# Two graph layers on one core: the table's rows fetched and weighted in three parts, and a rewritten steady list

## The chip, the core and the metric

The kernel runs on one core of a Trainium2 chip. The metric is the device time in microseconds (us) of one execution; the time of a kernel is the median of its runs. The core's engines each work through their own queue in order: TensorE (PE; PEld are its weight loads), VectorE (DVE), ScalarE (ACT), GpSimd (POOL) and SyncE (SP), which here issues DMAs only. They wait for each other through semaphores.

## What is computed

Input x has 32 batches of 512 channels by 1024 nodes; adj is 512 by 512. The reference, cut to what matters:

```python
def layer0(x, wq, wk, adj, bm):
    q = einsum('c,bcn->bn', wq, x)
    k = einsum('c,bcn->bn', wk, x)
    scores = q[:, None, :] + k[:, :, None]
    scores = where(scores > 0, scores, 0.01 * scores)
    att = softmax(scores, axis=-1)
    agg = einsum('bcn,bmn->bcm', x, att)
    return relu(einsum('oc,bcm->bom', adj, agg) + bm[None, :, None])

x = layernorm(x + layer0(x, wq, wk, adj, bm))
W = adj * adj
x = layernorm(x + einsum('bnf,nm->bmf', x, W) + bias)
```

## The kernel before

The score of a pair is a leaky ReLU of q + k, so the softmax needs no matrix of 1024 by 1024: with the nodes ranked by q, the nodes above a threshold get one exponential factor and those below another, and the weighted sum is a running sum from either end of the ranking. For each batch the kernel therefore does the following.

- **Projections p0 to p27** (`project`, L329): adj times x by a Strassen-like scheme with seven products, for two halves g of the nodes, in fp32. The order of the products is in `order` (L298): p0, p1 are P2, p2, p3 are P1, p4, p5 are P5, p6, p7 are P6, p8, p9 are P3, p10, p11 are P7 and p14, p15 are P4 of the first half; p12, p13 and p16 to p27 belong to the second half. Each accumulates into one of the PSUM banks A (P1, P6, P7, P4), B (P5, P3) and C (P2). A step named in NARROW (L934) issues its weights as two loads of 64 columns, each with its own matmul into half of the output; another issues one load of 128. Steps k (`keep`, L347) read a bank out to `zrow`, on ScalarE or VectorE: k0p1, k0p5, k0u2, k011, k022, k012 and k021 for the first half. Until k0p5 has copied P5 out of B, p8 and p9 may not accumulate there; p2 and p3 need A to be free of the batch before (`rd21`, the last read of the final product).
- **Ranking**: qb spreads q over the partitions, r0 to r7 (L403) count ranks on VectorE, sd0 to sd7 (L415) scatter the rows on GpSimd by indirect DMA into a table `td` in DRAM, c0 to c7 (L428) count thresholds on ScalarE.
- **Fetch** (fe, `fetch`, L454): SyncE reads the ranked rows back into `zs`, NB = 9 blocks of 60 rows for each half of the partitions. Block 8 takes two small DMAs (L461); the others come in three pairs (L466): blocks 0 and 1, block 7, blocks 2 to 6.
- **Weights of the table** (wx, wb): wx0 and wx1 (`weigh_exp`, L476, ScalarE, two Exp each) and wb0 and wb1 (`weigh_by`, L488 and L496, VectorE) make the triangular weights `lq`. Part 0 covers blocks 7, 8 and 0, 1 and part 1 the rest.
- **Table t0 to t8** (`table`, L510): running sums by matmul; step s takes block 8-s from above and block s from below. e (L522) evicts it on ScalarE, ca (ScalarE) and cp (GpSimd, both L528) carry its border rows into the next blocks, and ts (L536) stores it to `td` by DMA. A table step needs the carries of the step before, and so its e.
- **Gather** pi0 to pi7 (L543, GpSimd, indirect DMA) brings each node's three table rows into `rows`; oa, ox and no (L558 to L575) make the mixing factors; sc (L582, ScalarE) and ga, gb (L587, VectorE, "gains") mix the three.
- **Back**: u0 to u3 (L596) transpose the mixed rows, ad (L603) adds x, sq, rt, y (L612, L619, L628) are the first layer norm; rt is GpSimd's. u0 reads all eight node tiles, so it needs every gain.
- **Second layer**: T1 to T4 (L652) and m0 to m13 (L676) are a second Strassen-like product; m6, m7 need y2 and y3. rd reads the banks out, st, ro, sf, av (L705 to L729) are the second layer norm, so stores and ld loads the next x.

Nothing is scheduled by a tool here. Three lists written out by hand give the order of the program: BEGIN (L855), SLOT (L921), which is passed 28 times and where each step belongs to one of five batches in flight, and END (L885). Each engine gets its steps in the list's order; every engine waits in its own queue. The pool of PSUM has the banks A, B and C, and T for the table.

Of the kernel before, what the change touches and what calls it, by code (L numbers as in the profile page):

```python
# [23 lines left out]
def gat_gcn_resnorm_kernel(  # L24
# [25 lines left out]
    NB = N // R + 1  # L50
# [403 lines left out]
    def fetch(b):  # L454

        zd = tdb[b % 2].rearrange("(s u) c -> s u c", u=3)
        full = zd[0 : (NB - 1) * R, 0, :].rearrange("(j q p) c -> q p j c", q=2, p=RH)
        for half in range(2):
            r = (NB - 1) * R + half * RH
            n = min(RH, N - r)  # L460
            nc.sync.dma_start(  # L461
                out=zs[half * G + 1 : half * G + 1 + n, NB - 1, 0:ZW], in_=zd[r : r + n, 0, :]
            )
        for j0, j1 in ((0, 2), (NB - 2, NB - 1), (2, NB - 2)):
            for half in range(2):
                nc.sync.dma_start(  # L466
                    out=zs[half * G + 1 : half * G + 1 + RH, j0:j1, 0:ZW],
                    in_=full[half, :, j0:j1, :],
                )

    some_blocks = (((NB - 2, NB), (0, 2)), ((0, NB - 2), (2, NB)))
# [9 lines left out]
    def weigh_by(b, part, by=nc.vector):  # L481

        w = weights(b)
        for i, (j0, j1) in enumerate(some_blocks[part]):
            if part == 1:
                j0, j1 = max(j0, 1), min(j1, NB - 1)
# [7 lines left out]
        if part == 1:  # L494
# [267 lines left out]
    def also(role, name, f, *at):  # L762
        steps[name] = role, f, at
# [22 lines left out]
    also(1, "sx", share_exp)  # L786
    for h in range(2):
        also(1, f"wx{h}", weigh_exp, h)
        also(1, f"wb{h}", weigh_by, h)
# [72 lines left out]
    @0 fe @1 k022 p17 @0 sb1 @1 p14 k1p5 p15 @0 sb2 sg @1 p21 k021 p19 @0 c0 @1 p18 p20 k1p1 @0 c1 @1  # L862
    k111 p22 p23 @0 wx0 wb0 t0 @2 x11 @1 k1u2 @2 x12 @1 p25 @2 x03 @0 e0 @1 p24 k112 @0 ca0 ts0 cp0
    c2 t1 @1 k122 @0 wx1 @1 qb @0 wb1 e1 @1 p27 @0 ts1 @1 ql @0 cp1 @1 pk @0 c3 @1 p26 r0 @2 p4 @1
    k121 r1 @0 c4 @1 en @0 ca1 t2 @1 r4 @0 c5 @1 sd1 r5 @2 p5 @0 e2 ca2 @1 mx @0 ts2 cp2 @1 mr @0 c6
    @1 sd4 @0 t3 @1 r2 @2 p2 @1 sd0 r3 @0 e3 ca3 ts3 cp3 @1 r6 @0 t4 @2 p1 @1 sd5 r7 @0 e4 ca4 cp4
    @1 sd3 @0 t5 @2 p3 @1 sd7 @0 e5 ts5 @2 k0p1 @0 cp5 ca5 @1 sd2 @0 t6 @2 p0 @0 e6 @2 k0p5 @0 cp6
    ts6 @2 k011 @0 ca6 @1 sd6 @0 t7 @2 x13 x14 p6 @0 e7 @2 p7 @0 ca7 cp7 ts7 t8 ts4 @2 k0u2 p11 @0
    e8 c7 @2 p10 @0 ts8 @1 fe @0 sh @2 k022 x04 p14 @0 qw3 pi0 @2 p15 p9 @1 wx0 wb0 @2 k021 @1 c0 @2
    p18 @1 t0 c1 @2 p19 @1 c2 @2 p8 @1 e0 ca0 cp0 ts0 @2 k012 @1 c3 @0 pi2 @2 k1p1 @0 pi1 @2 p22 @0  # L870
    pi3 @2 p23 @0 pi7 @2 p17 @0 pi5 @2 k1u2 p16 @1 c4 @0 pi6 @1 t1 @2 k1p5 @1 wx1 @0 pi4 @2 p24 @1
    wb1 c5 @2 p20 p12 p25 p21 p13 @0 oa0 ox0 sx no0 @2 k122 @0 sc0 @2 k112 @1 e1 @2 p27 @0 ga0 sc2
    @1 ts1 ca1 cp1 @0 sc1 gb0 @1 t2 @0 ga1 gb1 @1 e2 @0 sc3 @2 k111 @1 cp2 ca2 @0 ga2 @1 t3 @0 ga3
    gb3 @2 p26 @0 oa1 @1 e3 @0 ox1 @1 cp3 @0 no1 gb2 sc4 sc5 ga4 sc6 ga5 @1 ca3 @0 ga6 sc7 @1 t4 @0
    gb5 @1 c6 @0 ga7 gb4 gb7 @1 e4 @0 gb6 u0 @1 ca4 ts4 @2 k121 @1 cp4 ts3 c7 @0 ad0 @1 t5 ts2 @0 u1
    @1 sh e5 @0 sq0 u2 @1 cp5 @0 ad1 @1 ca5 t6 @0 rt0 @3 ld0 @2 en @0 ad2 sq1 @2 pk @0 u3 @1 e6 @3
    ld1 @2 mx @1 ca6 cp6 @0 sB @2 mr @0 sq2 rt1 ad3 @1 t7 @0 qw5 @3 ld2 @1 e7 @0 sA @1 ts6 @0 rt2 y0
    @2 qb @1 ts5 cp7 ca7 @2 r0 @1 ts7 t8 @0 sq3 @2 r1 @1 e8 @0 rt3 y1 m1 @1 ts8 @2 r2 sd1 @3 ld3 @2
    ql r3 sd0 @0 y2 m0 @2 r4 sd2 @0 y3 m7 qw4 @2 c0 @1 pi3 @0 T1 m6 @2 c1 r5 @1 pi2 @0 rdp1 m2 @1
    pi1 @0 T2 @2 c2 r6 @1 pi0 @0 m5 @2 c3 @0 T3 m4 T4 @3 x01 @0 m3 @2 r7 @0 rdu2 rd11 m9 @2 sd7 @0  # L880
    rdp5 @1 sx @2 c4 sd5 @0 m8 @1 pi5 @0 m11 rd22 @2 sd4 @0 m10 @1 pi6 oa0 ox0 @2 c5 @1 no0 @2 sd3
    @0 m13 @3 x02 @1 sc2 @3 x03 @1 sc1 @2 sd6 @0 rd12 @1 sc0 @0 m12 @3 x04 @1 pi7 @0 rd21 @1 pi4 @2
    c6 c7 @1 sc3 @2 fe
# [5 lines left out]
    @28 st2 @29 sc6 @30 wx0 @31 p15 @29 sc7 @30 wb0 @28 ro2 @30 t0 @31 k021 @29 sc4 @28 ro1 sf2 @31  # L889
    x12 p18 @29 ga6 @30 e0 @31 p19 @30 ca0 @31 k012 @30 ts0 cp0 @29 gb3 @30 t1 @31 k1p1 @29 ga7 sc5  # L890
    @31 p16 @29 gb7 @30 e1 @31 p12 @28 sf1 @30 wx1 cp1 ts1 ca1 @31 p17 @30 wb1 @28 so3 av1 @30 t2
    @29 ga4 ga5 @31 p23 @30 e2 sh @31 p22 k1p5 @30 cp2 @31 k111 @30 ca2 t3 @29 gb4 @31 k1u2 @29 gb6
    @31 p25 @30 e3 @29 gb5 @30 ca3 @29 u0 @30 cp3 @28 av2 @30 t4 @29 ad0 @28 so2 @31 p24 @30 e4 @31
    x14 @30 ca4 @29 u1 @30 ts4 cp4 @31 k122 @29 sq0 @30 ts2 t5 @29 ad1 @28 so0 @31 p20 @30 e5 ca5
    @29 u2 @30 cp5 @29 sq1 @30 t6 @29 ad2 @31 p21 @30 e6 ca6 @29 u3 @30 cp6 ts6 @31 k112 @29 sq2 @30
    ts3 @31 pk @30 t7 @29 ad3 @28 so1 @31 p27 @30 ts5 e7 ca7 @31 mx @30 cp7 ts7 @31 qb mr @29 rt0
    @30 t8 @31 ql r0 @29 rt1 @31 p26 @30 e8 @31 r1 @29 sB @30 ts8 @31 k121 @29 y0 @31 en @29 sA @31
    r2 sd1 @29 sq3 @31 r3 sd0 @29 y1 m0 @30 pi3 @31 r4 c0 @30 pi2 @31 r5 @29 m1 @30 pi0 @29 T1 rt3
    @31 r6 @29 m2 rt2 @31 r7 sd2 @29 y2 m3 @31 sd3 @30 sx @29 rdp5 @30 pi1 @29 y3 m11 @31 sd5 @29
    rdp1 T2 @31 c1 sd7 @29 m5 @31 c2 sd6 @29 m7 @31 c3 sd4 @29 m10 @30 pi7 pi5 @29 m6 @30 oa0 ox0  # L900
    no0 @29 m4 T3 @30 sc3 sc0 @29 rd11 @31 fe @29 rdu2 T4 @31 c4 @29 m9 @30 sc2 @31 c5 @29 m8 @31 c6
    @29 rd22 @30 sc1 @31 c7 @29 rd12 m13 st0 @31 wx0 wb0 t0 @30 ga3 ga0 ga1 @31 e0 ca0 @29 st1 @31
    ts0 cp0 @30 pi6 @31 t1 @30 gb1 @29 m12 @31 e1 @30 gb3 @31 ca1 ts1 cp1 wx1 @29 ro0 @31 wb1 @29
    rd21 @31 t2 @30 pi4 ga2 @29 sf0 st2 @31 e2 ca2 cp2 t3 e3 ca3 cp3 @29 av0 ro1 @31 t4 @29 sf1 @30
    gb0 @31 e4 cp4 @30 oa1 ox1 @31 ca4 t5 @30 no1 gb2 sc4 sc5 ga4 sc7 ga5 @31 e5 @30 ga7 sc6 @31 cp5
    ca5 @30 ga6 @31 t6 @29 av1 @30 gb4 gb6 @29 so1 @30 gb5 @31 e6 @30 gb7 u1 @31 ca6 ts6 @29 st3 @31
    cp6 @29 ro2 @31 ts4 t7 ts2 @30 u0 @31 e7 ts3 ca7 @30 u3 @31 cp7 ts7 t8 @30 ad0 @31 ts5 e8 @30
    ad1 sq0 @31 ts8 @30 u2 @29 sf2 @31 sh @29 so0 @30 sq1 rt0 ad2 @31 sx @30 ad3 sq2 @31 pi0 @30 sA
    y0 rt1 @31 pi1 @30 y1 m1 @31 pi3 @30 sq3 T1 @31 pi2 @30 m0 rt2 sB rdp1 rt3 m3 y2 @31 pi7 @30 y3
    m7 @31 pi5 @30 T2 m6 @31 pi4 @30 T4 @31 pi6 @30 T3 m4 @29 ro3 @31 oa0 @30 m5 @31 ox0 no0 @30  # L910
    rd11 @31 sc2 @30 m2 rdu2 @31 ga2 sc3 @30 m9 @31 gb2 sc1 sc0 ga1 @30 rdp5 m8 @31 ga3 ga0 @29 av2
    @31 gb3 @30 m11 rd22 @31 gb0 @30 m13 @31 oa1 ox1 no1 @30 m12 @31 gb1 sc4 sc7 ga4 @30 m10 @31 sc5
    ga7 @30 rd21 @31 gb4 gb7 sc6 ga5 ga6 gb5 gb6 u0 @30 rd12 @31 u1 ad0 u2 sq0 ad1 u3 ad2 sq1 rt0
    ad3 sB y0 rt1 @30 st0 @31 sA y1 m0 @29 sf3 @31 sq2 @30 ro0 @31 T1 m1 sq3 rt2 m3 y2 rt3 y3 m2
    rdp1 T2 m6 rdp5 @30 st1 @29 av3 @31 m5 @30 sf0 st2 ro1 @31 m4 T4 @30 ro2 @31 T3 m7 rdu2 @30 sf1
    @31 rh110 @30 av1 st3 @31 m8 @30 so1 sf2 @29 so2 @30 ro3 av2 @29 so3 @31 m9 rh220 @30 av0 @31
    rh111 hb21 m10 rh221 @30 sf3 @31 hb31 @30 av3 @31 m11 rh120 @30 so3 @31 st0 @30 so0 so2 @31 m12
    rh121 ro0 st1 m13 rh210 sf0 hb20 ro1 av0 sf1 ag2 rh211 so0 ro2 av1 hb30 ag3 sf2 ro3 fa21 so1
    fa20 fo20 sf3 fa31 fa30 fo21 fo31 fo30
    """  # L920
    SLOT = """  # L921
    st1 p4 st0 p2 ga2 p5 ro0 st3 p3 p0 k0p1 ga0 k0p5 ro3 p1 st2 ro1 p7 ga3 p6 ro2 gb2 p8 sf3 k0u2
    sf0 ga1 av3 p10 gb0 k011 p11 x13 p12 oa1 k022 p9 ox1 av0 no1 p14 gb3 sc7 k012 p15 wx0 wb0 t0 x11
    k021 ga7 sc4 p19 sf1 gb1 e0 p17 ca0 ts0 sf2 cp0 sc6 x12 t1 av1 ga6 p16 gb6 e1 p18 wx1 cp1 ts1
    ca1 wb1 p13 so1 k1p1 sc5 t2 ga4 gb7 p22 e2 x14 p23 ca2 k111 cp2 ga5 t3 k1u2 k1p5 gb5 p24 gb4 e3
    ca3 u0 ts3 cp3 av2 so3 t4 ad0 so2 p21 so0 e4 ts2 ca4 u1 cp4 sq0 t5 ad1 p20 ld0 e5 ca5 u2 cp5 ts5
    sq1 rt0 t6 ad2 p25 ld1 rt1 e6 y0 u3 ts6 k122 cp6 k112 p26 ca6 pk ad3 sq2 t7 p27 e7 ld2 mx cp7
    ts7 k121 qb mr ca7 rt2 en ts4 y1 t8 r0 sA e8 r1 sB sq3 ts8 m0 sh sd0 ql ld3 T1 m1 c0 sd1 r2 m3
    rdp1 pi3 r3 y2 m2 rt3 r4 pi2 y3 m6 pi0 c1 T2 m7 sx pi1 T4 rdp5 c2 T3 m4 c3 pi5 r5 m5 r6 sd5 m11
# [47 lines left out]
```

## Times and profile before

| what | value |
|---|---|
| median of 3 runs | 2200.91 us (2197.12 to 2201.44) |
| the profiled execution: whole run | 2198.41 us |
| its span, first to last instruction | 2196.7 us |
| mean granted clock of TensorE | 0.99 |
| instructions | 35479 |
| DMA | 548.86 MB, mean 250 GB/s |

The page gives busy times and their share of the span by engine, then the chain of work that ended last: followed back from the last instruction, at each step to what released it. A timeline row has the start and the length in us, the engine, the line, the operation, the tile written and read with their shapes, the number of records, and in brackets the idle time before it and what ended that. A projection of fp32 leaves four records when its weights are 128 wide and eight when they are 64 wide; two 64-wide ones run side by side. Rows that overlap by a tenth or two are pipelined: compare starts with starts. A waits row has who waited for what, the total in us, how often, and the longest.

### The profile page before, as it was taken

The numbers are of one execution on the slowest core, as the hardware profiler recorded it, in microseconds if no ns is written. First come the engines' busy times: TensorE is split into PE (matmuls) and PEld (weight loads), VectorE is DVE, ScalarE is ACT, GpSimd is POOL, SyncE is SP. The second block draws the span as 40 slices with busy tenths as digits, with TensorE's granted clock in tenths as the row PEclk, the third lists the DMA queues.
The fourth block names the chain that finished last, engine by engine and source line by source line (L and its number), as shares of the span: only waits on it lengthen the run. The fifth ranks groups of instructions, "written<-read, shape, count | busy, mean of one in ns | idle before, by whom it ended". The sixth has DMA issues, their size and how long they took to land.

```text
span 2196.7 us, 35479 instructions
## 1 busy us (share of the span) xinstructions
PE 2102.5 (96%) x11697; PEld 1222.4 (56%) x11697; DVE 1775.9 (81%) x3576; ACT 1652.8 (75%) x2758; POOL 987.6 (45%) x1291
## 2 busy tenths in 40 slices
PE   7879999999999999999999999999999999999877
PEld 5446555556555556555656555556655556655433
DVE  7567888888888888888888898888888888888666
ACT  1577777887777887777888777878777788777765
POOL 1344455444445444445443445544445544445442
PEclk9999999999999999999999999999999999999998
DMA  7567888878888777888777889887888887888752
GB/s 250 166 229 252 264 266 281 257 239 254 268 260 277 262 247 244 268 246 286 266 250 234 265 253 282 273 249 233 262 265 267 282 252 236 258 265 264 221 205 96
DMA packets 179152, 548.86 MB, mean 250 GB/s; under 512 B 27404, under 2 KB 27416, under 8 KB 178968
## 3 DMA queue, kind: packets, MB, share of 16 engines
q1 hardware_dynamic: 121600, 277.06, 43.7%
q0 software_dynamic: 57344, 269.52, 34.3%
q8 instruction: 93, 1.52, 0.3%
q14 instruction: 91, 0.75, 0.1%
q10 hardware_dynamic: 24, 0.01, 0.0%
HBM read 338.17 MB, written 208.30 MB: 249 GB/s over the span
## 4 chain that ended last, share of the span: by engine, by line
PE 62%; ACT 12%; DVE 10%; issue 6%; DMA 6%; POOL 3%; SPq 1%; DVEq 0%; POOLq 0%; ACTq 0%
PE zp_A L338 18%; PE tp L510 10%; PE oA L676 9%; PE zp_B L338 8%; PE op L596 5%; PE zp_C L338 4%; DVE junk L403 4%; ACT y L628 4%; PE oB L676 3%; PE oC L676 3%; DMA zs<-td 2%; ACT rows L582 2%; ACT v L699 1%; POOL zs L528 1%; DMA td<-zs 1%
## 5 line engine op out<-in xcount | busy, mean ns | idle before, releaser
L587 DVE SCALAR_TENSOR_TENSOR rows<-rows,ra 128x512 f32<-128x512 f32 x512 | 366.2, 739 | 20.9 <-ACT rows L582 17.6
L676 PE MATMUL oA<-y,adj_sb 128*128 128x512 f32 x768 | 356.6, 607 | 9.8 <-ACT y L628 6.3
L415 POOL DMA_INDIRECT td<-zrow,ranki x256 | 269.3, 1052 | 213.7 <-DVE idx L439 80.0
L510 PE MATMUL tp<-zs,lq 128*64 128x257 f32 x2304 | 335.1, 392 | 27.2 <-POOL zs L528 16.3
L543 POOL DMA_INDIRECT rows<-td,idx x256 | 297.1, 1160 | 88.1 <-issue 68.0
L403 DVE SCALAR_TENSOR_TENSOR junk<-qb,zrow,first 128x1024 int8<-128x1024 f32 x240 | 307.1, 1279 | 10.9 <-PE qb L376 4.2
L528 POOL COPY zs<-ts 1x513 f32<-1x513 f32 x128 | 93.2, 728 | 474.4 <-ACT ts L522 474.3
L338 PE MATMUL zp_A<-wb,x 128*64 128x257 f32 (+1 forms) x1536 | 278.9, 388 | 12.6 <-issue 3.5
L428 ACT ACTIVATE junk<-lq,kc 128x1024 int8<-128x1024 f32 x240 | 274.4, 1143 | 2.0
L603 DVE SCALAR_TENSOR_TENSOR y<-op,nbm,x 128x1024 f32<-128x1024 f32 x128 | 163.8, 1282 | 127.4 <-PE op L596 127.2
L676 PEld LDWEIGHTS oA<-y,adj_sb 128*128 128x128 f32 x768 | 144.7, 193 | 191.7 <-issue 153.8
L510 PEld LDWEIGHTS tp<-zs,lq 128*64 128x64 f32 x2304 | 168.7, 136 | 135.6 <-POOL zs L528 37.8
L582 ACT ACTIVATE rows<-rows,ra 128x512 f32<-128x512 f32 x256 | 180.1, 718 | 77.5 <-DVE den L574 39.5
L359 ACT COPY zrow<-zp_A 128x514 f32<-128x514 f32 x192 | 112.8, 588 | 147.4 <-PE zp_A L338 130.1
L338 PEld LDWEIGHTS zp_A<-wb,x 128*64 128x64 f32 (+1 forms) x1536 | 177.0, 155 | 77.3 <-issue 25.1
L528 POOL COPY zs<-zs 1x513 f32<-1x513 f32 x128 | 78.3, 611 | 253.0 <-ACT zs L522 253.0
L628 ACT ACTIVATE y<-y,nb,r 128x1024 f32<-128x1024 f32 x128 | 158.9, 1241 | 4.3
L705 DVE BATCH_NORM_STATS2 st<-v 128x6 f32<-128x512 f32 x240 | 151.9, 674 | 0.0
L612 ACT ACTIVATE x<-y,nm 128x1024 f32<-128x1024 f32 x128 | 147.2, 1150 | 4.2
L729 ACT ACTIVATE v<-v,nb,rs 128x1024 f32<-128x1024 f32 x120 | 148.1, 1234 | 2.3 <-DVE nb L721 1.4
L596 PE MATMUL op<-ident,rows 128*128 128x128 f32 x1024 | 141.2, 282 | 4.6 <-DVE rows L587 2.6
L596 PEld LDWEIGHTS op<-ident,rows 128*128 128x128 f32 x1024 | 114.9, 143 | 46.1 <-issue 24.6
(162 smaller groups left out, 3784.6 us busy)
## 6 DMA issues: line engine op xcount, KB each, us to landing
x<-in_x_dram SPq DMA_DIRECT2D x128, 512.0 KB
out_dram<-v SPq DMA_DIRECT2D x120, 512.0 KB
zs<-td SPq DMA_DIRECT2D x64, 602.3 KB
td<-zs SPq DMA_DIRECT2D x288, 120.2 KB
td<-ts SPq DMA_DIRECT2D x224, 120.2 KB
zs<-td SPq DMA_DIRECT2D x64, 240.9 KB
zs<-td SPq DMA_DIRECT2D x96, 120.5 KB
td<-zs SPq DMA_DIRECT2D x8, 514.0 KB
```

The costliest lines, as they stand in the source:

```text
L338: nc.tensor.matmul(zp[n : n + wide, m, 0:CE], side(b, g, a)[:, c, m * P + n : m * P + n + wide], wb[:, w, c, :], start=first and c == 0, s ...
L403: nc.vector.scalar_tensor_tensor(junk(b)[:, 0:N], qbs[b], zrow[:, nt, 0:1], first[:, o : o + N], ALU.subtract, ALU.is_lt, accum_out=rank[: ...
L415: sc = nc.gpsimd.indirect_dma_start(out=td[:, :], out_offset=bass.IndirectOffsetOnAxis(ap=ranki[:, nt : nt + 1], axis=0), in_=zrow[:, nt, ...
L428: nc.scalar.activation(junk(b)[:, N : 2 * N], qs[b], AF.Sign, bias=kcs[b][:, nt : nt + 1], accum_out=signs(b)[:, nt : nt + 1],)
L510: nc.tensor.matmul(tp[i * G : (i + 1) * G, h, 0:CE], lw[:, ks[i], :], zs[:, j, 1 + h * CE : 1 + (h + 1) * CE], start=True, stop=True,)
L528: copy(zs[row : row + 1, to, 1:ZW], ts[row : row + 1, 0 : ZW - 1])
L543: nc.gpsimd.indirect_dma_start(out=rows[:, mt, :], out_offset=None, in_=tdb[b % 2].rearrange("(s u) c -> s (u c)", u=3), in_offset=bass.In ...
L582: nc.scalar.activation(u, u, AF.Copy, scale=ratios(b)[:, k, 1:2])
L587: nc.vector.scalar_tensor_tensor(u, rg[:, k, i, 1 : C + 1], ratios(b)[:, k, i : i + 1], u, ALU.mult, ALU.add)
L596: nc.tensor.transpose(op[:, mt * P : (mt + 1) * P], rg[:, mt, 1, 1 + ot * P : 1 + (ot + 1) * P], ident)
L628: nc.scalar.activation(yall[:, ot], yall[:, ot], AF.Identity, bias=nb, scale=r)
L676: nc.tensor.matmul(o[:, m, :], quarters[w][:, a, m * P : (m + 1) * P], part(b, y)[:, a, :], start=fresh and a == 0, stop=a == CT // 2 - 1, ...
```

## The change

Three things are changed together. The fetch comes in four pairs of DMAs instead of three: block 0; blocks 6 and 7; blocks 1 and 2; blocks 3 to 5. The weights come in three parts: part 0 covers blocks 8 and 0, what t0 alone reads; part 1 blocks 6, 7 and 1, 2; part 2 the rest. And SLOT and NARROW are rewritten; in BEGIN and END only the new steps are put in (wx1 and wb1 follow t0, and what was wx1 and wb1 is wx2 and wb2).

```diff
-        for j0, j1 in ((0, 2), (NB - 2, NB - 1), (2, NB - 2)):
+        for j0, j1 in ((0, 1), (NB - 3, NB - 1), (1, 3), (3, NB - 3)):
...
-    some_blocks = (((NB - 2, NB), (0, 2)), ((0, NB - 2), (2, NB)))
+    some_blocks = (
+        ((NB - 1, NB), (0, 1)), ((NB - 3, NB - 1), (1, 3)), ((0, NB - 3), (3, NB)),
+    )
...
-            if part == 1:
+            if part == 2:
                 j0, j1 = max(j0, 1), min(j1, NB - 1)
...
-        if part == 1:
+        if part == 2:
...
+    for i in range(3):
+        also(1, f"wx{i}", weigh_exp, i)
+        also(1, f"wb{i}", weigh_by, i)
     for h in range(2):
-        also(1, f"wx{h}", weigh_exp, h)
-        also(1, f"wb{h}", weigh_by, h)
```

The SLOT list before and after, whole, with NARROW:

```diff
-    st1 p4 st0 p2 ga2 p5 ro0 st3 p3 p0 k0p1 ga0 k0p5 ro3 p1 st2 ro1 p7 ga3 p6 ro2 gb2 p8 sf3 k0u2
-    sf0 ga1 av3 p10 gb0 k011 p11 x13 p12 oa1 k022 p9 ox1 av0 no1 p14 gb3 sc7 k012 p15 wx0 wb0 t0 x11
-    k021 ga7 sc4 p19 sf1 gb1 e0 p17 ca0 ts0 sf2 cp0 sc6 x12 t1 av1 ga6 p16 gb6 e1 p18 wx1 cp1 ts1
-    ca1 wb1 p13 so1 k1p1 sc5 t2 ga4 gb7 p22 e2 x14 p23 ca2 k111 cp2 ga5 t3 k1u2 k1p5 gb5 p24 gb4 e3
-    ca3 u0 ts3 cp3 av2 so3 t4 ad0 so2 p21 so0 e4 ts2 ca4 u1 cp4 sq0 t5 ad1 p20 ld0 e5 ca5 u2 cp5 ts5
-    sq1 rt0 t6 ad2 p25 ld1 rt1 e6 y0 u3 ts6 k122 cp6 k112 p26 ca6 pk ad3 sq2 t7 p27 e7 ld2 mx cp7
-    ts7 k121 qb mr ca7 rt2 en ts4 y1 t8 r0 sA e8 r1 sB sq3 ts8 m0 sh sd0 ql ld3 T1 m1 c0 sd1 r2 m3
-    rdp1 pi3 r3 y2 m2 rt3 r4 pi2 y3 m6 pi0 c1 T2 m7 sx pi1 T4 rdp5 c2 T3 m4 c3 pi5 r5 m5 r6 sd5 m11
-    x01 rdu2 sd4 x02 c4 r7 m8 pi4 rd11 sd3 m9 sd7 oa0 m10 rd22 ox0 sd6 no0 m12 sd2 x04 sc2 x03 c5
-    rd12 m13 pi7 sc0 pi6 sc3 rd21 c6 sc1 c7 fe
+    st0 p5 st1 p4 ro0 p3 sf0 ga0 av0 p2 st3 p0 k0p5 k0p1 p9 gb0 st2 p6 p7 ga3 p1 ro2 k0u2 ga2 gb3
+    p11 sf2 k011 p10 ga1 wx0 p13 k022 p8 oa1 x11 ox1 av2 p14 no1 p15 wb0 sc5 k012 t0 gb1 k021 sc7
+    gb2 p19 x12 e0 p18 sc4 ga7 ts0 wx1 p16 cp0 ca0 wb1 ro1 ga4 k1p1 t1 sc6 ga5 p12 ga6 e1 p17 ca1
+    cp1 ts1 k111 wx2 gb4 t2 so0 ro3 wb2 p23 e2 gb6 p22 ca2 sf3 cp2 x13 t3 k1u2 x14 av3 p24 gb7 e3
+    gb5 u0 ca3 sf1 cp3 k1p5 t4 ad0 av1 p21 so1 e4 ts2 ca4 u1 cp4 sq0 ts3 t5 ad1 so3 ts4 p25 rt0 e5
+    p20 ca5 ts5 k122 cp5 sq1 u2 k112 pk t6 y0 ad2 ld1 so2 p27 e6 u3 ca6 cp6 ts6 sq2 rt1 t7 ad3 p26
+    ld2 e7 mx cp7 ts7 k121 qb mr ca7 rt2 en ld0 y1 t8 r0 sA sB e8 r1 m1 sq3 ts8 sh sd1 m0 sx ld3 T1
+    y2 sd0 r2 m3 ql pi1 c0 r3 m2 rt3 r4 pi2 y3 m7 pi0 rdp1 T2 c1 m6 pi3 r5 rdp5 pi5 T4 m4 rd11 sd2
+    m5 x01 sd5 T3 m11 rdu2 r6 sd3 c2 m9 x02 sd4 c3 r7 m8 c4 sd7 oa0 m10 pi7 rd22 ox0 c5 no0 sd6 m13
+    c6 rd12 pi6 sc3 x03 m12 c7 x04 pi4 sc0 rd21 sc1 sc2 fe
...
-    NARROW = "p1 p6 p7 p8 p9 p10 p11 p12 p13 p14 p16 p17 p18 p19 p20 p22 p23 p24 p25 p27"
+    NARROW = "p1 p8 p10 p11 p12 p14 p15 p19 p17 p16 p18 p13 p22 p23 p24 p21 p20 p25 p26 p27"
```

On ScalarE a pass of SLOT has 64 steps instead of 63 and on VectorE 68 instead of 67; SyncE issues two more DMAs a pass. The products, the matmuls and the bytes moved are the same.

## What was predicted, and how

> All times are of the profiled execution (span 2196.7 us, whole run 2198.4 us). The median of the runs is 2200.9 us, 2.5 us above it; the sum below is made on 2198.4 and carried to the runs by adding that 2.5.
>
> **What bounds the kernel now.** I read the page first: busy shares and the chain that ended last.
>
> ```profile
> PE 2102.5 (96%) x11697; PEld 1222.4 (56%) x11697; DVE 1775.9 (81%) x3576; ACT 1652.8 (75%) x2758; POOL 987.6 (45%) x1291
> PE 62%; ACT 12%; DVE 10%; issue 6%; DMA 6%; POOL 3%; SPq 1%; DVEq 0%; POOLq 0%; ACTq 0%
> ```
>
> TensorE is busy 96% and holds 62% of the chain. So a steady slot costs its matmuls plus the places where TensorE starts one late. The 28 passes of SLOT are nearly equal: the starts of the mx transpose lie 64.95 us apart in most passes and 65.4 on average. I took one pass of 64.95 us and read the TensorE timeline; S = 1617.53 is where its projections start.
>
> ```profile
> 1614.10 3.60 PE L676 MATMUL oA<-y,adj_sb 128*128 128x512 f32 x8
> 1617.53 1.03 PE L338 MATMUL zp_B<-wb,y 128*128 128x257 f32 x4
> 1618.79 1.14 PE L338 MATMUL zp_A<-wb,x 128*128 128x257 f32 x4 [0.23 <-issue]
> 1619.77 1.03 PE L338 MATMUL zp_B<-wb,y 128*128 128x257 f32 x4
> 1620.64 1.03 PE L338 MATMUL zp_A<-wb,x 128*128 128x257 f32 x4
> ...
> 1629.51 2.10 PE L338 MATMUL zp_A<-wb,x 128*64 128x257 f32 x12
> 1631.54 1.09 PE L510 MATMUL tp<-zs,lq 128*64 128x257 f32 x8
> 1632.46 1.04 PE L338 MATMUL zp_A<-wb,x 128*64 128x257 f32 x8
> 1633.33 1.04 PE L338 MATMUL zp_B<-wb,rows 128*64 128x257 f32 x8
> 1634.52 1.09 PE L510 MATMUL tp<-zs,lq 128*64 128x257 f32 x8
> ```
>
> Read starts against starts. A projection or table step, wide (4 records) or narrow (8), takes 0.87 when the next follows at once (1619.77 to 1620.64). Three places take longer: p4 at the head (1.26, then p2 0.97), p14, p15 and t0 at the end (0.97, 1.07, 0.92, each with a change of weight width beside it), and p17 ahead of t1 (1.19). The same steps are late by the same amounts in every undisturbed pass. Next, ScalarE and GpSimd around t0:
>
> ```profile
> 1630.27 0.65 ACT L476 ACTIVATE w<-zs,bw,el 128x2 f32<-128x2 f32 x2
> 1631.65 0.59 ACT L359 COPY zrow<-zp_A 128x514 f32<-128x514 f32 x1 [0.72 <-PE zp_A L338]
> 1632.13 0.73 ACT L582 ACTIVATE rows<-rows,ra 128x512 f32<-128x512 f32 x1
> 1632.76 0.58 ACT L522 COPY ts<-tp 128x514 f32<-128x514 f32 x1
> 1633.37 0.62 ACT L528 COPY zs<-ts 1x513 f32<-1x513 f32 x1
> ```
>
> A table step can start only after the step before has been evicted (e) and its two border rows carried (ca, cp). Here ca0 ends at 1633.99, cp0 at 1634.46, t1 starts at 1634.52. Last, the fetch: the trace's completions for this pass put its last piece that part 0 of the weights needs at 1629.57 (S+12.0). ScalarE reached wx0 at 1630.27 and did not wait; over all passes that last landing lies between S+11 and S+14, and in some of them wx0 waits:
>
> ```profile
> ACT w L476 <- DMA zs<-td: 12.4, 10, 6.1
> ```
>
> **The change part by part.**
>
> *Head of the slot, and the narrow list.* p2 writes bank A, and must wait for rd21, ScalarE's copy out of A (it ends at 1618.74, p2 starts at 1618.79). The new order p5 p4 p3 p2 puts two steps on bank B first, so A is wanted at S+1.74 and free near S+1.3: p4's excess 0.40 and p2's 0.11 go. Two more counts (c6, c7) stand ahead of rd21, 1.14 each, but fall into 2.62 and 2.18 that ScalarE idles just before, around ox0. p9 moves to sixth place; its accumulation must wait for k0p5, which now stands behind av0 on ScalarE. That chain: VectorE st0 ends S+0.8, GpSimd's ro0 takes 1.27 (0.61, 0.08, 0.57), sf0, av0 1.24, k0p5 0.59: S+4.1. p9 is wanted at S+4.3. It is hidden, with 0.2 to spare; without that cover it costs what av0 is late.
> p15 becomes narrow between p14 and t0, which are narrow: two changes of width go, and with them the excess 0.10+0.20 of p14 and p15. Counted over the slot there are 13 changes instead of 15. So t0 comes 0.40+0.11+0.30 = 0.80 earlier, at S+13.2.
>
> *Fetch in three parts.* Bytes and packets are the same; SyncE issues ten DMAs instead of eight (0.3 to 0.7 each in this pass), beside the transfer. In this pass the piece for block 8 landed at S+8.6, and later pieces of 60 rows 0.5 to 0.7 after the last, of 120 rows 1.0 to 1.2. So part 0 lands near S+9.6, part 1 near S+14.0, the rest as now, near S+17.5.
> The landings 0.5 to 0.7 apart bound what one more piece can cost the last part, 0 to 0.7; since the packets are the same I take 0. Against the split speaks the Trainium skill's page DMA: Bandwidth & Descriptors (Rules for kernel authors; Anatomy of one DMA): coalesce, since each DMA pays about 2.0 us fixed. If queued pieces paid that one after the other, two more would by this estimate bring the last part 4 us later, 2 us after wx2 wants it, and the slot would lose 1.5 instead of gaining 0.5; the landings above disagree.
> wx0 now stands at about S+7.8 on ScalarE and will wait some 2 us there; behind it are ox1, av2, sc5 and then k021, which isn't ready before S+13.3. They need 0.65+0.21+1.13+0.63 = 2.6, done at S+12.3: hidden, unless part 0 lands after S+10.6.
>
> *A third pair of Exp, three more VectorE products.* 0.65 on ScalarE a slot. On VectorE 128-wide products step 0.20 to 0.29 and 384-wide 0.67 and 0.54; a 64-wide one lies between a 12-wide (0.17) and these, I take 0.20, a 320-wide one between 0.28 and 0.73, I take 0.5; together +0.3 (bounds 0 to 0.8).
>
> *t0 to t3.* Three steps now lie between t0 and t1 and two between t1 and t2. For TensorE t0 to t1 would be 4 x 0.868 = 3.47. But ScalarE now has k021, sc7, e0, sc4, wx1, ca0: starting 0.2 after t0, at steps of 0.49, 0.63, 0.47, 0.63, 0.71 and 0.62, ca0 ends 3.76 after t0's start; t1 at 3.82. Before it was 2.98 (bound by cp0). t1 to t2 is 2.61 instead of 3.52. So t0 to t2 is 6.43 instead of 6.50: -0.07. What stands behind wx1 on ScalarE is ca0, and t1 waits for that; wx1 itself needs part 1 by S+15.6, against S+14.0. t2 to t3 stays 2.61.
>
> *t3 to t4.* New: av3 stands ahead of e3. From p22's end, 0.2 after t3's start: k1u2 0.49, av3 1.13, e3 0.62, ca3 0.62, so t4 can start 3.15 after t3; TensorE would come at 2.90: +0.25. Similarly sq1 and y0 ahead of e6 make t7 about 0.1 late.
>
> *u0.* It needs every gain. VectorE runs from 1616.84 to 1642.72 with two idle times, read here:
>
> ```profile
> 1634.77 1.54 DVE L587 SCALAR_TENSOR_TENSOR rows<-rows,ra 128x512 f32<-128x512 f32 x2 [0.76 <-ACT rows L582]
> 1636.67 1.21 DVE L488 TENSOR_TENSOR lq<-tri,w 128x384 f32<-128x384 f32 x2 [0.36 <-ACT w L476]
> ...
> 1640.54 2.18 DVE L587 SCALAR_TENSOR_TENSOR rows<-rows,ra 128x512 f32<-128x512 f32 x3
> ```
>
> Its work is 25.88-1.12 = 24.76, plus 0.3: done at 1641.9 if it never idles. TensorE comes to u0 at S+24.1 = 1641.65, and needs the last gain 0.54 into it, 1642.2. It fits with 0.3 to spare.
>
> *u0 to the next slot.* The same steps with as many changes of width. From qb on nothing shortens: first ranks, two sends, one gather, rt3, y3, then the second half of m6 (now m7):
>
> ```profile
> 1596.13 1.02 POOL L415 DMA_INDIRECT td<-zrow,ranki  x1 [0.31 <-DMA td<-zs]
> 1597.46 1.06 POOL L543 DMA_INDIRECT rows<-td,idx  x1 [0.30 <-issue]
> 1598.54 0.25 POOL L619 TENSOR_SCALAR r<-sq 128x1 f32<-128x1 f32 x1
> ```
>
> rt3 ends at 1599.46, y3 starts at 1599.51 and m6 waits 0.37 for it. The new list moves y2 forward but leaves rt3 behind two sends and a gather: no gain.
>
> *Sum a slot:* -0.80-0.07+0.25+0.1 = -0.52; 28 slots -14.6. The passes above 64.95 sum to 11 us; about half have wx waiting for the fetch, and part 0 now has more room: -3. In the opening list wx0 waits 6.1 once; its part is now some 0.4 of the bytes: -2 (bounds 0 to -4). In the closing list t0 waited 0.74, but wx1 now stands ahead of e0: 0. Together -19.6: 2178.8, and 2181 on the runs' scale.
>
> **Rivals.**
> 1. *More comes through.* The waits at t4 and t7 don't come, for instance because av3 and y0 run in idle time: 28 x 0.35 = 10 more, 2171; with t1 at TensorE's own 3.47 another 10, 2161. Against it: ScalarE has no idle time ahead of e0 in the rows above.
> 2. *VectorE takes over at u0.* If it idles in the new order as it did (1.12), the last gain comes 0.8 later, and the slot gains nothing: 2196 to 2205.
> 3. *Slower: the first gather waits for the table's last rows.* pi1 reads what ts8 stores; ld0 (512 KB) is now issued between ts7 and ts8, and so2 just ahead of ts6. rt3 is behind pi1, and y3 behind rt3, so each us of delay is a us of slot. The price is in two passes of before: the first gather started 1.11 and 1.44 after the send instead of 0.30, and these passes took 65.73 and 66.07. It decides from 0.5 late; at 1.1 the slot loses 0.58: +16, less 2, so 2215. For it speaks that the lateness hits the chain from qb directly; against it, that ts8 is issued no sooner and no later than before.
> 4. *The split doesn't do what it says.* Part 1 lands after S+15.6 (the late passes of before ran 1.5 behind); then wx1 blocks ca0 and t1, 0.9 late gives +0.4 a slot (2210), 1.4 late +0.9 (2224). Against it: in this pass part 1 has 1.6 of room.
>
> **How the numbers follow.** Forecast (2174 to 2189) 0.45; rival 1 0.13; rival 2 0.10; rival 3 0.19; rival 4 0.13. Rivals 1 and the forecast are faster by over 0.2% (4.4 us, about what a measurement of this kernel can tell from no change): 0.58. Same 0.10, slower 0.32. The range from 2166 to 2218 leaves out half of rival 1 and the far ends of 3 and 4, some 2 in 10. The forecast's own range is 2174 to 2189.
>
> **What would show it.** In the new profile: no wait at the third projection; p15, t0 without excess; t0 at S+13.2; t1 3.8 after t0; t4 0.25 late; wx0 waiting some 2 us for zs at no cost; passes near 64.4. A gap over 0.30 ahead of the first gather would show rival 3, a wait of the second Exp pair for zs rival 4, u0 waiting on rows rival 2.

## The result, and the profile after

The changed kernel takes **2276.19 us** (median of 4 runs, 2276.03 to 2282.76), the kernel before 2201.18 beside it (4 runs): the ratio is 1.0344, with an interval of 1.031 to 1.0378. The prediction was 2181, faster; the kernel is 75 us slower, and outside the range. The profiled execution has a span of 2274.2 us and a mean granted TensorE clock of 0.972, where it was 0.99.

The page of the new kernel, for busy times, the granted clock in 40 slices, and the chain that ended last:

```profile
PE 2122.9 (93%) x11697; PEld 1246.6 (55%) x11697; DVE 1803.8 (79%) x3640; ACT 1672.5 (74%) x2822; POOL 1016.8 (45%) x1291
PEclk9989999999999999999999999999999999999988
PE 68%; ACT 9%; DVE 8%; DMA 6%; issue 4%; POOL 3%; SPq 0%; POOLq 0%; DVEq 0%; ACTq 0%
```

TensorE issues as many matmuls as before, is busy 20 us longer, and yet its share falls from 96% to 93%: the same work runs slower somewhere, and there is idle time besides. (The clock's row doesn't show it: a slice is 57 us long.) The waits of the new kernel (who waited for whom, us in total, times, longest) name the idle time:

```profile
POOL rows L545 <- issue: 77.3, 195, 4.1
PE oC L678 <- ACT y L630: 65.9, 30, 3.8
...
ACT nb L629 <- POOL r L622: 58.9, 29, 5.4
```

About once a pass TensorE waits some 2 us for y on ScalarE, ScalarE waits for GpSimd's root r, and GpSimd has a gap ahead of a gather (`rows`). In the kernel before, ScalarE waited 8.3 us in all for that root:

```profile
ACT nb L627 <- POOL r L620: 8.3, 6, 5.2
```

One pass of the new kernel, whose mx is at 1034.59, shows the links. SyncE, GpSimd, ScalarE and TensorE in turn:

```profile
1035.76 0.43 SPq L131 DMA_DIRECT2D x<-in_x_dram  x1
1038.03 1.56 SPq L538 DMA_DIRECT2D td<-zs  x2
```
```profile
1040.44 1.02 POOL L415 DMA_INDIRECT td<-zrow,ranki  x1 [0.31 <-issue]
1043.84 1.05 POOL L545 DMA_INDIRECT rows<-td,idx  x1 [2.37 <-issue]
1044.90 0.26 POOL L621 TENSOR_SCALAR r<-sq 128x1 f32<-128x1 f32 x1
1045.25 0.57 POOL L622 TENSOR_TENSOR r<-r,mhalf 128x1 f32<-128x1 f32 x1
```
```profile
1045.85 0.29 ACT L629 ACTIVATE nb<-nm,r 128x1 f32<-128x1 f32 x1 [1.73 <-POOL r L622]
1046.18 1.24 ACT L630 ACTIVATE y<-y,nb,r 128x1024 f32<-128x1024 f32 x1
```
```profile
1044.30 1.02 PE L678 MATMUL oC<-y,adj_sb 128*128 128x512 f32 x2
1047.47 3.20 PE L678 MATMUL oC<-y,adj_sb 128*128 128x512 f32 x4 [2.15 <-ACT y L630]
```

Read it upwards. TensorE has done the first half of m7 and waits 2.15 for y3; y3 waits for rt3 (1045.25); rt3 stands behind the first gather (1043.84); and the gather starts 2.37 after the second send instead of 0.30. The gather reads what ts8 stores. In the pass of the kernel before that the prediction read, TensorE went through both products with no gap over 0.15, and on SyncE's queue ts7, ts4 and ts8 (two DMAs each) followed ld2 with no load between them:

```profile
1599.99 3.97 PE L676 MATMUL oC<-y,adj_sb 128*128 128x512 f32 x8
```
```profile
1589.88 0.36 SPq L131 DMA_DIRECT2D x<-in_x_dram  x1
1590.35 4.11 SPq L536 DMA_DIRECT2D td<-zs  x6
```

By the trace's completions ts8, issued by 1039.59, landed at 1042.73, behind the load ld0 of 512 KB issued at 1035.76, which landed at 1041.26. Over the steady passes the last of ts8's bytes lands 4.00 us after its issue (median), where it was 1.73. The profile's own label for the gap ("issue", in other passes "DMA x<-in_x_dram") is no help here; the second run below settles which transfer it is.

The last row has a second thing: four records take 3.20, 0.8 each, where a record takes 0.43. The stretches of this pass (us, busy times of TensorE, its weight loads, VectorE, ScalarE and GpSimd, then the granted clock, the DMA share and GB/s) show why:

```profile
1044.00:1047.20 3.20, 1.32 (x4) 0.25 (x2) 1.57 (x5) 1.44 (x4) 2.85 (x4) 1.00 0.67 209
1047.20:1050.60 3.40, 3.13 (x5) 1.34 (x6) 3.12 (x5) 3.15 (x5) 2.50 (x3) 0.63 0.96 343
```

Right behind the idle time (from 1048.1 in this pass) the granted clock falls to one half for 3.4 us. That happens in 17 of the 27 whole steady passes, and in none before. The passes with it last 68.0 to 70.8, those without it 66.0 to 66.8, but for one of 68.0 in which m13 waited too (1.64).

Split at S, where the projections start, the passes say where the time is (means of 27 passes, us):

| | before | after |
|---|---|---|
| S to the next mx | 37.92 | 37.09 |
| mx to the next S | 27.42 | 30.74 |
| pass | 65.35 | 67.84 |

What the change was forecast to shorten did shorten, by 0.83. The other half, of which the prediction said "no gain", lost 3.32.

### The profile page after: what moved, and what is told of

Same layout as the page of the kernel before. It is cut to its first block, busy times and chain, and to the rows that moved or that the text cites. A ratio compares the mean times of both kernels' runs of the same rounds, so it can differ in the third digit from the quotient of the medians.

```text
span 2274.2 us, 35789 instructions
## 1 busy us (share of the span) xinstructions
PE 2122.9 (93%) x11697; PEld 1246.6 (55%) x11697; DVE 1803.8 (79%) x3640; ACT 1672.5 (74%) x2822; POOL 1016.8 (45%) x1291
## 4 chain that ended last, share of the span: by engine, by line
PE 68%; ACT 9%; DVE 8%; DMA 6%; issue 4%; POOL 3%; SPq 0%; POOLq 0%; DVEq 0%; ACTq 0%
PE zp_A L338 16%; PE oA L678 15%; PE tp L512 10%; PE zp_B L338 8%; PE oB L678 5%; PE oC L678 5%; PE op L598 5%; PE zp_C L338 5%; ACT y L630 3%; DMA x<-in_x_dram 3%; DVE rows L589 2%; POOL rows L545 2%; ACT x L614 1%; DVE junk L403 1%; DMA td<-zs 1%
## 5 line engine op out<-in xcount | busy, mean ns | idle before, releaser
L415 POOL DMA_INDIRECT td<-zrow,ranki x256 | 288.3, 1126 | 221.9 <-DVE idx L439 81.4
L545 POOL DMA_INDIRECT rows<-td,idx x256 | 279.9, 1093 | 146.9 <-issue 77.3
L530 POOL COPY zs<-ts 1x513 f32<-1x513 f32 x128 | 114.0, 890 | 372.0 <-ACT ts L524 371.9
L338 PE MATMUL zp_A<-wb,x 128*64 128x257 f32 (+1 forms) x1792 | 254.3, 383 | 5.2 <-DVE zrow L357 2.5
L678 PE MATMUL oC<-y,adj_sb 128*128 128x512 f32 x256 | 154.7, 738 | 66.1 <-ACT y L630 65.9
L701 ACT COPY v<-oA 128x1024 f32<-128x1024 f32 x90 | 90.5, 1005 | 153.9 <-PE oA L678 140.2
L338 PEld LDWEIGHTS zp_A<-wb,x 128*64 128x64 f32 (+1 forms) x1792 | 156.5, 145 | 75.9 <-ACT zrow L359 9.1
```

The source lines that it names most:

```text
L338: nc.tensor.matmul(zp[n : n + wide, m, 0:CE], side(b, g, a)[:, c, m * P + n : m * P + n + wide], wb[:, w, c, :], start=first and c == 0, s ...
L415: sc = nc.gpsimd.indirect_dma_start(out=td[:, :], out_offset=bass.IndirectOffsetOnAxis(ap=ranki[:, nt : nt + 1], axis=0), in_=zrow[:, nt, ...
L530: copy(zs[row : row + 1, to, 1:ZW], ts[row : row + 1, 0 : ZW - 1])
L545: nc.gpsimd.indirect_dma_start(out=rows[:, mt, :], out_offset=None, in_=tdb[b % 2].rearrange("(s u) c -> s (u c)", u=3), in_offset=bass.In ...
L678: nc.tensor.matmul(o[:, m, :], quarters[w][:, a, m * P : (m + 1) * P], part(b, y)[:, a, :], start=fresh and a == 0, stop=a == CT // 2 - 1, ...
```

## The experiments

All ratios are against the kernel before, run beside them on the same chip: 2200.21 us beside runs 1 to 4, 2200.95 beside 5 to 8, 2202.38 beside 9 to 12, so times of different sets compare to some 2 us. m7 (m6 before) takes 1.72 when nothing is late; what it takes beyond that, a lower clock included, is called its excess. In the diffs, lists are cut to the place of the edit.

**1. rt3 ahead of the first gather.**

```diff
-    y2 sd0 r2 m3 ql pi1 c0 r3 m2 rt3 r4 pi2 y3 m7 ...
+    y2 sd0 r2 m3 ql rt3 pi1 c0 r3 m2 r4 pi2 y3 m7 ...
```

> The new kernel with rt3 moved ahead of the first gather (pi1) in SLOT; nothing else. Theory A (the loss is GpSimd's order: the gather waits for the table's last rows, rt3 stands behind it, y3 behind rt3, m7's second half behind y3; the drops of TensorE's granted clock follow from that idle time): m7 loses its median excess of about 3.5 us a pass, the clock stays at 0.99, passes of 64.1 to 64.6, time 2172 to 2190. Theory B (y3 is late for another reason, such as ql and c0 ahead of it on ScalarE, or late ranks): passes stay above 66, time 2240 to 2276. Theory C (the clock drops of themselves, for instance because TensorE's work lies closer together, and make the wait look long): the wait shrinks but the clock stays near 0.972 and the time above 2225.

2204.25 us, ratio 1.001 (0.9993 to 1.0026); clock 0.986. One step moved past one gather takes back 72 of the 75 us. m7's excess is 0.57 in nearly every pass instead of 2.8 (medians), two windows of half clock are left in the steady passes instead of 17, and the best passes last 64.5. So theory A holds for the chain, B and C fall, but the time is 14 above A's range: the mean pass is 65.4. What is left is read on VectorE, in a pass of 66.1 us:

```profile
447.16 0.16 DVE L560 TENSOR_TENSOR s<-rows,kc 128x4 f32<-128x4 f32 x1 [2.82 <-DMA rows<-td,idx]
```

The own scores (oa0) wait for the gathers, which are still late, and rd22 and m13 stand behind them.

**2. ld0 after ts8, GpSimd's order as in the new list.**

```diff
-    ... rt2 en ld0 y1 t8 ... m1 sq3 ts8 sh ...
+    ... rt2 en y1 t8 ... m1 sq3 ts8 ld0 sh ...
```

> The new kernel with the load ld0 (512 KB) issued after the last table store ts8 instead of just ahead of it; GpSimd's order stays. Theory A with ts8 queued behind the load: the first gather starts again 0.3 to 1 us after the sends, m7 waits less than 1 us, the clock stays up, time 2180 to 2205. Theory D (the gather waits for the load itself, since it waits on a semaphore that the load raises, and not for ts8's rows): ld0 now lands later still, the gather with it, time 2276 or more. If so2, issued ahead of ts6, is what delays ts8: only part of the wait goes, 2215 to 2260.

2209.89, ratio 1.0042 (1.0025 to 1.0058), 5 above A's range and 5 below that for so2's share. ts8 lands 2.84 after its issue instead of 4.00, m7's excess is 1.3 instead of 2.8 (medians), and one window of half clock is left. Theory D falls on one pass: there ld0 landed at 427.22, ts8 at 424.83, and the gather started at 425.89, before the load had landed. It is ts8's rows that the gather waits for.

**3. The old list with the fetch and weights in three parts.**

```diff
-    ... p15 wx0 wb0 t0 x11 k021 ... p18 wx1 cp1 ts1 ca1 wb1 ...
+    ... p15 wx0 wb0 t0 wx1 wb1 x11 k021 ... p18 wx2 cp1 ts1 ca1 wb2 ...
```

> The new kernel (fetch and weights in three parts, its opening and closing lists) with the old SLOT and NARROW; wx1 wb1 stand right behind t0 and wx2 wb2 where the second pair was. It tells the split from the list. Theory A (all of the loss is the list's): 2195 to 2215, the upper end if wx1 ahead of e0 makes t1 0.5 late in each pass (28 x 0.5 = 14). Theory S (the split itself, two more pieces of the fetch, costs the loss): 2240 or more.

2220.47, ratio 1.0094 (1.0064 to 1.0123). Five above A's range, far below S: the split alone does not make the loss, though placed like this it costs 20 us. The mean pass is 65.79; 12 of the 20 are in the steady passes, the rest ahead of and behind them. It is t1 that comes late: 2.81 to 6.33 after t0, where it was 2.66 to 3.04. The second pair of Exp stands ahead of e0 here and waits for its part of the fetch, as in the slowest pass:

```profile
1253.25 0.39 ACT L478 ACTIVATE w<-zs,bw,el 128x2 f32<-128x2 f32 x1 [1.96 <-DMA zs<-td]
```

That is the wait of rival 4, in the old list.

**4. The kernel before with ld0 just ahead of ts8.**

```diff
-    ... t5 ad1 p20 ld0 e5 ... rt2 en ts4 y1 ... sq3 ts8 ...
+    ... t5 ad1 p20 e5 ... rt2 en ts4 y1 ... sq3 ld0 ts8 ...
```

> The kernel before with one thing changed: ld0 issued just ahead of ts8 instead of between ts2 and ts5. Theory A (a 512 KB load ahead of ts8 delays the gather, and rt3 behind it): the wait at m6's second half grows from 0.4 us by 0.8 to 2.5 a pass, with drops of the granted clock where TensorE idles over some 2 us: 2223 to 2300. Theories B and C (the queue of loads is not at fault): 2201 plus or minus 5.

2250.52, ratio 1.021 (1.0184 to 1.0236). One load moved in the old list makes most of the loss: ts8 lands 3.62 after issue (1.73), m6's excess grows from 0.37 to 2.02, and the granted clock drops in six of the 27 passes (all last 66.1 to 69.0). Theory A, from the other side.

**5. Both edits: rt3 ahead of the gather, ld0 after ts8.**

> The new kernel with both edits of the first two runs: rt3 ahead of the first gather, and ld0 after ts8. With rt3 moved alone the pass came to 64.5 us at best and 65.4 on average; what was left was VectorE, where the own scores (oa0) waited for the late gathers and rd22 behind them, so that m13 or the projections started late. Theory A (ts8's rows are late because 512 KB transfers stand ahead of them, and the gather is late with them): that wait goes too, passes of 64.5 to 64.9, time 2178 to 2192. Rival: the gathers are late for the work on GpSimd itself, ld0's place counts for nothing once rt3 is moved: 2200 to 2208.

2187.42, ratio 0.9928 (0.991 to 0.9945). Passes of 64.5 to 65.6, mean 64.66. This is the change as it was forecast, with its fault taken out; moving rt3 brings no gain of its own that shows, since mx to the next S takes 27.52, and 27.42 before. VectorE's waits for the gathered rows fall to 22.6 us in all, from 50.6 in run 1. For the page's lines above:

```profile
PE 2090.2 (96%) x11697; PEld 1233.2 (56%) x11697; DVE 1799.9 (82%) x3640; ACT 1669.6 (76%) x2822; POOL 1025.6 (47%) x1291
PE 67%; DVE 12%; ACT 9%; DMA 6%; issue 3%; POOL 2%; SPq 1%; POOLq 0%; DVEq 0%; ACTq 0%
```

TensorE's busy time falls by 32.7 us against the new kernel, with the same matmuls: that much of the loss was the clock, by this count.

**6. The same, with y3 ahead of c0 and so2 early.**

```diff
-    ... t2 so0 ro3 ... ad2 ld1 so2 p27 ... ql rt3 pi1 c0 r3 m2 r4 pi2 y3 m7 ...
+    ... t2 so0 so2 ro3 ... ad2 ld1 p27 ... ql rt3 y3 pi1 c0 r3 m2 r4 pi2 m7 ...
```

> The same, and also y3 ahead of the first count c0 on ScalarE, and the store so2 (512 KB) issued behind so0, well ahead of the last table stores. m7's second half still waited 0.57 us for y3 when rt3 was moved. If ScalarE's order is all that is left there, m7's excess of 0.57 goes: passes of 64.0 to 64.3, 28 x 0.5 = 14 below the kernel with both edits: 2162 to 2180. Rival: the wait moves on (VectorE's ranks, or the copies rdp1, rd11 behind the later c0, become late): no change against the kernel with both edits, or up to 10 more.

2180.65, ratio 0.9899 (0.988 to 0.9917): the fastest version, 1% below the kernel before. ts8 lands 1.99 after issue, m7's wait is gone, most passes are 64.2. It gains 7, not 14: in a few passes m13 is still late, and in one of them (67.9) the clock drops there too.

**7. TensorE kept busy while it waits.** The new kernel as it is, with two products between the halves of m7.

```diff
+            if i == 7 and a == 0 and 1 <= b < B - 3:
+                for _ in range(2):
+                    nc.tensor.matmul(
+                        o[:, 0, :], quarters[w][:, 0, 0:P], part(b, y)[:, 0, :],
+                        start=True, stop=True, skip_group_check=True,
+                    )
```

> The new kernel with its list as it is, and two products more in each pass between the halves of m7 (written to the bank half that m6 overwrites from its start; 0.43 us a record, 1.7 us a pass): TensorE works for most of the time in which it waited for y3. The wait itself stays. Theory A2 (about half of the loss is the drop of the granted clock that follows an idle time of TensorE of 2 us or more): no drops, passes of 66.0 to 66.5 instead of 67.8, time 2222 to 2240. Theory C (the drops come of themselves): 2270 to 2285, or more by up to 28 x 1.7.

2240.81, ratio 1.0174 (1.0152 to 1.0197), at the upper end of A2 and far below C. 48 us of matmuls were added (28 x 1.72), and the kernel is 35 us faster than the new kernel without them. ScalarE's wait for the root is as long as it was:

```profile
ACT nb L629 <- POOL r L622: 55.7, 29, 5.4
```

but no window of half clock is left in the steady passes. So the drops follow from the idle time, and they cost some 35 of the 72 us that moving rt3 gave back (run 5's busy time says 33, and the windows of the new kernel's steady passes sum to 68 us, 34 lost at half speed); the rest is the wait itself.

**8 and 11. The new list without the split** (both edits of run 5, two parts, the first pair just ahead of t0). In run 8 the second pair stood behind t2, so t2 took the weights of the pass before; in run 11 it stands ahead of it.

```diff
-    ... wx0 p13 k022 p8 ... p15 wb0 sc5 k012 t0 ... wx1 p16 cp0 ca0 wb1 ... wx2 gb4 t2 so0 ro3 wb2 ...
+    ... p13 k022 p8 ... p15 sc5 k012 wx0 wb0 t0 ... p16 cp0 ca0 ... e1 wx1 p17 cp1 ts1 ca1 wb1 k111 gb4 t2 ...
```

> The new list with both edits (rt3 ahead of the gather, ld0 after ts8), but with the fetch and the weights in two parts as before, the first pair of Exp just ahead of t0, none between e0 and ca0, and the old opening and closing lists. It is the list without the split. If the split brings what the prediction said (no waits of wx0 for the fetch, but t1 0.8 later and t2 0.9 earlier): this takes 0 to 10 more than the kernel with both edits. If the split costs (t1's wait): up to 14 less.

> The list without the split, now with the second pair of weights ahead of t2, as the old list had them (in the first version of this run they stood behind t2, so that t2 took the weights of the pass before, and its output isn't the reference's). rt3 ahead of the gather, ld0 after ts8. The passes of the first version took 65.6 against 64.5 with the split: so the split is worth at least 1 us a pass in the new list. With t2 waiting for its weights: 2215 to 2235. If the old result came from t2's wrong place alone: 2185 to 2200.

2216.98 (ratio 1.0066, 1.0047 to 1.0086) and 2230.98 (1.0132, 1.0114 to 1.0151), against 2187.42 with the split. Run 8 is 20 above what was expected, run 11 within its first range. But this isn't a clean price of the split. The groups of run 11 show t0 waiting for VectorE's weights, and those for ScalarE's Exp:

```profile
L510 PE MATMUL tp<-zs,lq 128*64 128x257 f32 x2304 | 360.8, 396 | 53.7 <-DVE lq L488 21.8 <-POOL zs L528 21.7 <-issue 6.2
L488 DVE TENSOR_TENSOR lq<-tri,w 128x384 f32<-128x384 f32 (+1 forms) x128 | 55.9, 461 | 44.7 <-ACT w L476 44.7
```

The Exp waits only 11.2 us in all for the fetch. It is late by the place that was chosen for it: in a pass of run 11 ox1 ahead of it waits 3.43 for VectorE's oa1, av2 and sc5 follow, and wx0 starts at 1060.04 for a t0 that TensorE could have started at 1060.28. So what the split is worth alone stays open: with the old list it cost 20 as placed in run 3, and in the new list a better place for two parts was not tried.

**9 and 10. oa0 behind rd22**, on the version of run 6 and on that of run 1.

```diff
-    ... sd7 oa0 m10 pi7 rd22 ox0 c5 ...
+    ... sd7 m10 pi7 rd22 oa0 ox0 c5 ...
```

> The kernel of rt3, ld0, y3 and so2 moved, and one more move: VectorE's own scores oa0, which wait for the gathered rows, go behind the copy rd22. In some passes of the version before, m13 was up to 2 us late behind that copy, and one pass took 67.9. If VectorE's order is the cause, those passes fall to 64.2 and the mean with them from 64.5 to 64.25: 7 less, 2170 to 2176. Rival: ox0, no0 and the combine weights behind oa0 become late instead and the gains of the next pass with them: no gain, 2178 to 2185.

> The new kernel with rt3 ahead of the first gather and oa0 behind rd22; ld0 and so2 stay ahead of ts8, so the gathers stay late. Theory A (a late gather costs nothing by itself: only what stands behind it on GpSimd and behind its readers on VectorE costs): most of the 0.9 us a pass that was left above 64.5 goes, 2180 to 2192. If the late gathers cost by other ways too (their rows wanted by the combine): 2195 to 2206.

2206.22 (ratio 1.0022, 1.0011 to 1.0034) and 2224.14 (1.0104, 1.0089 to 1.012): 26 and 20 slower than without, and above every range that was given for them. m13 is never late now, but every pass is, by the same amount (65.3 and 65.9): ScalarE's ox0 waits for oa0, and behind it c5 to c7 and rd21 are late, so that p3 waits for bank A. ScalarE and TensorE in run 9:

```profile
1027.40 0.21 ACT L567 ACTIVATE ac<-s 128x4 f32<-128x4 f32 x1 [2.23 <-DVE s L561]
```
```profile
1033.31 2.00 PE L338 MATMUL zp_A<-wb,x 128*128 128x257 f32 x8 [0.85 <-ACT v L701]
```

The rival of run 9 had the kind of mishap right (what stands behind oa0 becomes late) and ox0 among the late steps, but not the step that it reached, rd21, nor its price.

**12. so2 early, ld0 and rt3 as in the new list.**

```diff
-    ... t2 so0 ro3 ... ad2 ld1 so2 p27 ...
+    ... t2 so0 so2 ro3 ... ad2 ld1 p27 ...
```

> The new kernel with one move: so2, a store of 512 KB that stood just ahead of ts6, goes behind so0. ld0 stays between ts7 and ts8, rt3 behind the first gather. If each 512 KB ahead of ts8 delays the gather alike: about half of what moving ld0 gave (66), 2235 to 2250. If only the transfer right ahead of ts8 counts: 2265 to 2278.

2232.79, ratio 1.0138 (1.0108 to 1.0167): 43 us below the new kernel, just under the first range. ts8 lands 3.36 after issue. The new list issues so2, ts6, ld2, ts7, ld0, ts8 in this order. So a store of 512 KB with four other steps between it and ts8 delays ts8 too (0.64, against 1.16 for ld0): more of the queue's backlog counts than the neighbour alone.

## Why the prediction was wrong, point by point

- **Head of the slot and the narrow list: right.** t0 stands at S+13.18 in all but two passes, against 14.02 before and 13.2 forecast; the excess of p4, p2, p14 and p15 is gone.
- **t0 to t2: right in sum, off in its parts.** t0 to t1 takes 3.52 (forecast 3.82), t1 to t2 2.87 (2.61); together 6.39, a gain of 0.12 (forecast 0.07): two errors that cancel, by luck. Not forecast: t2 to t3 takes 2.93 instead of 2.61.
- **t3 to t4 and t7: half right.** t4 is 0.12 late, not 0.25; t4 to t7 is unchanged (9.67, before 9.69).
- **u0: right.** No wait of u0 for the gains beyond what it had (its step is 1.07, before 1.02): rival 2 did not come.
- **Fetch: right in effect.** The Exp pairs wait 36.2 us in all for the fetch, before 12.4, and that hides: t0 to t1 never varies, so rival 4 did not come with the new list (it did in run 3). In run 5 the three parts land at S+10.1, 14.7 and 17.2 (medians; forecast 9.6, 14.0, 17.5), and the last one landed at S+17.7 before. So the two more pieces did not bring the last part 4 us later, as the prediction's estimate from the Trainium skill's page DMA: Bandwidth & Descriptors would have it; that page's section (Anatomy of one DMA) gives its 2.0 us for DMAs issued from GpSimd, and SyncE issues these. The packets were not quite the same: 960 more in all, each under 512 B.
- **Sum of S to mx:** -0.64 in the median pass, where the whole slot was forecast at -0.52.
- **From qb on: this step failed.** It put the wait of the first gather for ts8 at nothing. The prediction said "From qb on nothing shortens" and "no gain" and left it there; and against rival 3 it said that "ts8 is issued no sooner and no later than before". That was true of the issue (done 4.2 after mx in both kernels), and beside the point: what mattered was the queue ahead of it. The landing of ts8 after its issue, 1.73 before and 4.00 with ld0 and so2 ahead, was never worked out against the gather. In the kernel before, the gather starts 1.27 after ts8's last landing; where it waits (new kernel) 1.11. So the slack was some 0.2 us, and 2.27 more of landing used it up at once: the gather starts 2.46 after the send instead of 0.30 (medians), and the half from mx to the next S lost 3.32 a pass.
- **Rival 3 named the mechanism**, in the right order (ld0 and so2 ahead, gather, rt3, y3), at 0.19 and at a price of 0.58 a slot. Its size was read from two passes of before with a late gather (0.8 and 1.1 late); these were passes of the old queue. The lateness came to 2.2, and TensorE's clock about doubled what it cost, for which the prediction had no term. No steady pass of before shows such a drop, since TensorE idled at most 1.2 us at this place; but the same profile has ten stretches of half clock ahead of and behind the steady passes, nine of them behind 1.7 us or more of idle time within 3.4 us.
- **Opening and closing: wrong by 10.** Forecast -2. With the fault taken out (run 5) the time up to the fourth mx grows by 4.5 us and that from the last mx but one on by 3.1. The 27 steady passes between give -18.5 (forecast -17.6 for 28), so the span falls by 10.8, not by 20. Where these 7.6 us arise was not traced.

Run 5 shows what the forecast was worth otherwise: 2187 against 2181, inside its own range of 2174 to 2189. It is rt3's and ld0's places in the new list that turned 13 us of gain into 75 of loss.

## What to carry to other kernels

When a list is rewritten, write out SyncE's queue too, old beside new, and for each store that something on the critical chain reads, compare its landing with the reader's start: the slack is landing to start less what the reader takes at best, here 0.2 us, and each big transfer put ahead ate into it. Keep small steps that others wait for ahead of an instruction that waits on a transfer, on the same engine. And price a wait of TensorE that reaches about 2 us at up to twice its length, as it came to here, or put matmuls into it.

## What the runs showed of the hardware

- **The clock after a short idle time.** In the new kernel TensorE idles 1.5 to 3.8 us at m7 in each pass. The half-clock windows behind it are 3.4 or 6.8 us long, and the passes with one of 3.4 last some 2 us longer. What decides is how the idle time lies: in every trace here the changes of the granted clock lie on one grid of 3.413 us, whose start differs from run to run against the passes. Counted by the stretches of that grid, over the steady passes of all fourteen kernels, a stretch at full clock with 2.0 us or more of idle TensorE was always followed by one at half clock, one with less than 1.88 never; from 1.88 to 1.99 both occur. So an idle time of 2.66 in run 12 (at 761.9, cut by the grid into 0.84 and 1.82) was followed by none, and one of 1.95 in run 4 (at 765.1, within one stretch) was. Ahead of and behind the steady passes, with other work on TensorE, less was enough at times (1.16 in the kernel before).
- The Trainium skill's page TensorE: Matmul & The Clock Gate gives as the rule that TensorE should have no idle gaps over about 3.4 us (HAM oscillation — how this bites in real kernels), and says of the window, 3413 ns long, that it runs freely (What's actually happening). The grid above agrees with the length; the threshold doesn't for this kernel: 2 us of idle time in a window that was otherwise busy were enough, by the passes above and run 7.
- **Filling a wait with useless matmuls can pay**: 48 us of them made the kernel 35 us faster (run 7).
- **From a landing to the gather that waits for it**: medians of 1.06 to 1.12 us in the seven kernels where it waited in most passes (the new kernel, runs 1, 2, 4, 7, 10 and 12).
- The page DMA: Bandwidth & Descriptors (Queues, rings and completion order) says that each DMA engine takes one queue's descriptors in order. The runs agree: ts8's landing, 4.00 after issue, falls to 3.36, 2.84 and 1.99 as so2, ld0 and both are taken from ahead of it (runs 12, 2 and 6), though run 6 differs in other steps as well.
